# Four graph layers on one core: all units as one stream of chunk pairs, with tails and next queries emitted step by step between VectorE's passes

## Chip, cores, metric

One core of one Trainium2 chip. The metric is the device time of one execution in microseconds (us). All runs quoted here are in the fast state, so no difference below comes from a slower state of the chip. Experiments came on three chips; each was timed against the kernel before on its own chip. Engine names as in the profile: PE is TensorE (PEld its weight loads), DVE VectorE, ACT ScalarE, POOL GpSimd. L571 is line 571 of the kernel profiled.

## What is computed

16 graphs share one random adjacency matrix of 1024 nodes (density 1/128) and have 128 features each. Four layers run one after the other: layers 0, 2 and 3 are attention over the neighbours (8 heads of 16) with a feed-forward part, layer 1 is a simpler graph attention with one score per edge.

```python
def attention_layer(adj, h, ...):                   # L0, L2, L3
    Q, K, V = h @ Wq, h @ Wk, h @ Wv                # 8 heads of 16
    s = einsum(Q, K) / sqrt(16);  s = where(adj == 0, -inf, s)
    x = layer_norm(h + softmax(s) @ V @ Wo + bo)
    return layer_norm(x + relu(x @ W1 + b1) @ W2 + b2)
def graph_layer(x, adj, ...):                       # L1
    h = x @ W;  e = leaky_relu(h @ a_src [:, None] + h @ a_dst [None, :])
    e = where(adj == 0, -inf, e)
    return layer_norm(softmax(e) @ h + x)
```

## The kernel before

Nodes are sorted by degree. Keys and values (the graph layer: features and a score) are written per layer to a table in DRAM, and rows are fetched with indirect DMAs, here called **gathers**. A **chunk** is one gathered row for each of 128 places: four neighbours of 32 nodes. A **unit** is one layer, one half of the graphs, one tile of 128 nodes: 64 units. A unit has between 3 and 10 **pairs of chunks**; a pair is one gather buffer, `[128, 2, 2048]` floats in an attention layer. Before its passes a unit needs its **query replicas**: each node's query, copied to the places of its four neighbours. The unit's end, here called the **tail**, runs once for each of two halves `h` of four graphs. Cut to what the argument touches:

```python
def attention(l, g, t):
    # query, replicated over the rows of a chunk: PE, then ACT copies
    for h in range(HF): ...                 # q = x @ Wq;  qr[j//2][:, j%2, cols] = rep_j @ q
    for r, n in enumerate(ROUNDS[t]):
        for jp in range((n + 1) // 2):
            e, m = gathered(l, g, t, r, jp)                               # POOL issues
            nc.vector.tensor_tensor(e[..ROW], e[..ROW], qr[jp], ALU.mult)   # DVE 2.29 us
            nc.vector.tensor_reduce(sc, e[..ROW], X, ALU.add)               # DVE 2.28 us
            nc.scalar.activation(x, sc, AF.Exp, scale=...)                  # ACT
            nc.vector.tensor_tensor(v, v, x, ALU.mult)                      # DVE 2.28 us
        summed(t, r, acc, pairs, ROW)                                       # PE
    rec = divisors(t, es_by_round, G * H)
    for h in range(HF):                     # the tail of each half, in one go
        o = acc * rec;  oT = turned(o);  ps = oT @ Wo + x (by the identity)
        nc.vector.tensor_tensor(y, ps, bo, ALU.add);  z = normed(y)
        x1 = turned(z); f1 = relu(x1 @ W1 + b1); ps = f1 @ W2 + x1 (by the identity)
        nc.vector.tensor_tensor(y, ps, b2, ALU.add)
        finish(l, g, t, h, normed(y), ...)  # next layer's projection, or the output

def normed(y):
    ... bn_stats, bn_aggr on DVE -> mv
    nc.gpsimd.tensor_scalar(rstd, mv[:, :, 1], EPS, None, ALU.add)
    nc.gpsimd.tensor_tensor(rstd, rstd, power, ALU.pow)
    nc.vector.scalar_tensor_tensor(shift, mv[:, :, 0], -1.0, rstd, ALU.mult, ALU.mult)
    ... z = y * rstd + shift on ACT
# driver: for each layer, graph half and tile: attention(l, g, t) or graph_attention(l, g, t)
```

Of the kernel before, what the change touches and what calls it, by code (L numbers as in the profile page):

```python
# [20 lines left out]
P = 128  # L21
# [40 lines left out]
NC = len(CHUNK)  # L62

# [9 lines left out]
def sparse_path(ctx: ExitStack, tc: tile.TileContext, a: dict, out: bass.AP, flag):  # L73
# [227 lines left out]
    gathers = ctx.enter_context(tc.tile_pool(name="gathers", bufs=4))  # L301
    reps = ctx.enter_context(tc.tile_pool(name="reps", bufs=2))
# [3 lines left out]
    exps = ctx.enter_context(tc.tile_pool(name="exps", bufs=7))  # L306
# [7 lines left out]
    srcs = {}  # L314

    def project(l, g, t, h):

        table = tables[l, g][t * P : (t + 1) * P, :]
        if LAYERS[l][1] is ATTN:
            kv = twos.tile([P, 2, GH, D], F32, tag="kv", name="kv")  # L320
            for i in range(0, GH, 2):
                ps = bank([P, 2, 2 * D])
                for k in range(2):
                    nc.tensor.matmul(  # L324
                        ps[:, k, :], xT[g, t, h][:, i + k, :], w[LAYERS[l][0], "Wkv"],
                        start=True, stop=True,
                    )
                nc.scalar.copy(
                    kv[:, :, i : i + 2, :].rearrange("p c g d -> p g c d"),
                    ps.rearrange("p g (c d) -> p g c d", d=D),  # L330
                )
            nc.sync.dma_start(
                table.rearrange("p (c x) -> p c x", c=2)[:, :, h * GH * D : (h + 1) * GH * D],
                kv.rearrange("p c g d -> p c (g d)"),
            )
            return
# [3 lines left out]
        for i in range(0, GH, 2):  # L340
# [7 lines left out]
            nc.vector.tensor_copy(  # L348
# [3 lines left out]
            nc.vector.tensor_copy(  # L352
                srcs[g, t][:, at : at + 2].rearrange("p (g o) -> p g o", o=1), ps[:, :, D + 1 :]
            )

# [3 lines left out]
    def normed(y):  # L359
# [3 lines left out]
        for i in range(GH):  # L363
            nc.vector.bn_stats(st[:, i, :], y[:, i, :])  # L364
            nc.vector.bn_aggr(mv[:, i, :], st[:, i, :])  # L365
# [4 lines left out]
        nc.vector.scalar_tensor_tensor(shift, mv[:, :, 0], -1.0, rstd, ALU.mult, ALU.mult)  # L370
# [21 lines left out]
    def gathered(l, g, t, r, jp):  # L392
        n = min(2, ROUNDS[t][r] - 2 * jp)
        width = tables[l, g].shape[1]
        e = gathers.tile([P, 2, width], F32, tag="e", name="e")
        for k in range(n):
            nc.gpsimd.indirect_dma_start(  # L397
                out=e[:, k, :], out_offset=None, in_=tables[l, g][:, :],
                in_offset=bass.IndirectOffsetOnAxis(ap=idx[:, t, 2 * jp + k, r : r + 1], axis=0),
            )  # L400
        return e, n

    def summed(t, r, acc, es, base):

        n = ROUNDS[t][r]
        for h in range(HF):
            for j in range(n):
                nc.tensor.matmul(  # L408
                    acc[32 * j : 32 * j + 32, h, :],
                    marks[:, CHUNK[t, r, j], :],  # L410
                    es[j // 2][:, j % 2, base + h * GH * D : base + (h + 1) * GH * D],
                    start=(r == 0), stop=last_round(t, j) == r,
                )

    def last_round(t, j):
        return max(r for r, n in enumerate(ROUNDS[t]) if n > j)

    def divisors(t, ps_by_round, width):
        den = accs.tile([P, width], F32, tag="den", name="den")
        for r, n in enumerate(ROUNDS[t]):  # L420
            for j in range(n):
                nc.tensor.matmul(  # L422
                    den[32 * j : 32 * j + 32, :], marks[:, CHUNK[t, r, j], :],
                    ps_by_round[r][:, j, :],
                    start=(r == 0), stop=last_round(t, j) == r,
                )
        both = smalls.tile([P, 2, width], F32, tag="both", name="both")
        nc.scalar.copy(both[:, 0, :], den)
        nc.vector.reciprocal(both[:, 1, :], both[:, 0, :])
        nc.gpsimd.tensor_tensor(seen[:, :, :width], seen[:, :, :width], both, ALU.add)  # L430
        return both[:, 1, :]

    def attention(l, g, t):
        layer = LAYERS[l][0]
        p = {n: w[layer, n] for n in ("Wq", "Wo", "bo", "W1", "b1", "W2", "b2", "ln1_g", "ln1_b", "ln2_g", "ln2_b")}
        xt = [xT[g, t, h] for h in range(HF)]
        qr = [reps.tile([P, 2, ROW], F32, tag="qr", name="qr") for _ in range(J // 2)]
        for h in range(HF):
            q = ones_.tile([P, GH * D], F32, tag="q", name="q")
            ps = bank([P, GH, D])  # L440
            for i in range(GH):
                nc.tensor.matmul(ps[:, i, :], xt[h][:, i, :], p["Wq"], start=True, stop=True)
            nc.scalar.copy(q, ps.rearrange("p g d -> p (g d)"))
            cols = slice(h * GH * D, (h + 1) * GH * D)
            pss = []
            for j in range(J):
                ps = bank([P, GH * D])
                nc.tensor.matmul(ps, rep_of(j), q[32 * j : 32 * j + 32], start=True, stop=True)
                pss.append(ps)
            for j in range(J):  # L450
                nc.scalar.copy(qr[j // 2][:, j % 2, cols], pss[j])  # L451

        acc = accs.tile([P, HF, GH * D], F32, tag="acc", name="acc")
        es_by_round = []
        for r, n in enumerate(ROUNDS[t]):
            ex = exps.tile([P, J, G * H], F32, tag="ex", name="ex")
            pairs = []
            for jp in range((n + 1) // 2):
                e, m = gathered(l, g, t, r, jp)
                nc.vector.tensor_tensor(  # L460
                    e[:, :m, :ROW], e[:, :m, :ROW], qr[jp][:, :m, :], ALU.mult
                )
                sc = smalls.tile([P, 2, G * H], F32, tag="sc", name="sc")
                nc.vector.tensor_reduce(  # L464
                    sc[:, :m, :],
                    e[:, :m, :ROW].rearrange("p k (a d) -> p k a d", d=HD),
                    mybir.AxisListType.X, ALU.add,
                )
                x = ex[:, 2 * jp : 2 * jp + m, :]
                nc.scalar.activation(x, sc[:, :m, :], AF.Exp, scale=1.0 / HD**0.5)  # L470
                v = e[:, :m, ROW:].rearrange("p k (a d) -> p k a d", d=HD)
                nc.vector.tensor_tensor(  # L472
                    v, v,
                    x.rearrange("p k (a o) -> p k a o", o=1).to_broadcast([P, m, G * H, HD]),
                    ALU.mult,
                )
                pairs.append(e)
            summed(t, r, acc, pairs, ROW)
            es_by_round.append(ex)
        rec = divisors(t, es_by_round, G * H)  # L480
        xnew = []
        for h in range(HF):
            o = twos.tile([P, GH, D], F32, tag="o", name="o")
            nc.vector.tensor_tensor(
                o.rearrange("p g (a d) -> p (g a) d", d=HD),
                acc[:, h, :].rearrange("p (a d) -> p a d", d=HD),
                rec[:, h * GH * H : (h + 1) * GH * H]
                .rearrange("p (a o) -> p a o", o=1)
                .to_broadcast([P, GH * H, HD]),
                ALU.mult,  # L490
            )
            oT = twos.tile([P, GH, P], F32, tag="oT", name="oT")
            turned(o, oT)
            ps = bank([P, GH, D])
            for i in range(GH):
                nc.tensor.matmul(ps[:, i, :], oT[:, i, :], p["Wo"], start=True, stop=False)  # L496
                nc.tensor.matmul(ps[:, i, :], xt[h][:, i, :], ident, start=False, stop=True)  # L497
            y = twos.tile([P, GH, D], F32, tag="y", name="y")
            nc.vector.tensor_tensor(y, ps, over_graphs(p["bo"]), ALU.add)  # L499
            z = normed(y)  # L500
            x1 = twos.tile([P, GH, P], F32, tag="oT", name="x1")
            turned(z, x1, p["ln1_g"], p["ln1_b"])
            f1 = ones_.tile([P, F, GH * P], F32, tag="f1", name="f1")
            for f in range(F):
                ps = bank([P, GH * P])
                nc.tensor.matmul(  # L506
                    ps, p["W1"][:, f * P : (f + 1) * P], x1.rearrange("p g n -> p (g n)"),
                    start=True, stop=True,
                )
                nc.scalar.activation(f1[:, f, :], ps, AF.Relu, bias=p["b1"][:, f : f + 1])  # L510
            ps = bank([P, GH, D])
            for i in range(GH):
                for f in range(F):
                    nc.tensor.matmul(  # L514
# [531 lines left out]
```

## Time and profile before

| | before |
|---|---|
| time, median of 4 runs | 5873.0 us (5865.0 to 5879.9) |
| profiled span, mean clock of PE | 5874.2 us, 0.69 |
| PE, DVE, ACT, POOL busy | 52, 43, 21, 21% |
| unit of 4 pairs, attention | 95.6 us, DVE busy 36.6 |

The prediction reads one unit closely. Two more views are needed for what follows. The first is the table of windows with one line for each layer (columns: window; length; busy us and number of instructions of PE, PEld, DVE, ACT, POOL; clock; DMA share; GB/s). The layers end where VectorE takes the last reciprocal of their last unit; the first begins with the first large pass.

```profile
334.00:1921.70 1587.70, 820.65 (x3376) 426.14 (x3376) 710.85 (x1023) 335.16 (x705) 284.93 (x296) 0.67 0.29 110
1921.70:2672.90 751.20, 439.70 (x1846) 235.63 (x1848) 300.41 (x655) 143.63 (x358) 236.38 (x246) 0.67 0.42 138
2672.90:4308.60 1635.70, 843.18 (x3456) 429.45 (x3448) 703.15 (x927) 358.96 (x726) 296.37 (x307) 0.70 0.31 116
4308.60:5811.90 1503.30, 754.87 (x3184) 371.96 (x3184) 707.60 (x947) 308.59 (x652) 376.14 (x379) 0.67 0.31 119
```

The list of waits (who waited for what: total us, times, longest us):

```profile
DVE y L520 <- PE ps L518: 1005.5, 96, 11.3
DVE e L460 <- ACT qr L451: 650.4, 48, 189.1
DVE y L499 <- PE ps L497: 502.0, 96, 9.9
```

These are the two y steps of the tails and the query replicas: 2158 us of VectorE's idle time, 189 of them the one wait at the start.

### The profile page before, as it was taken

The numbers are of one execution on the slowest core, as the hardware profiler recorded it, in microseconds if no ns is written. First come the engines' busy times: TensorE is split into PE (matmuls) and PEld (weight loads), VectorE is DVE, ScalarE is ACT, GpSimd is POOL, SyncE is SP. The second block draws the span as 40 slices with busy tenths as digits, with TensorE's granted clock in tenths as the row PEclk, the third lists the DMA queues.
The fourth block names the chain that finished last, engine by engine and source line by source line (L and its number), as shares of the span: only waits on it lengthen the run. The fifth ranks groups of instructions, "written<-read, shape, count | busy, mean of one in ns | idle before, by whom it ended". The sixth has DMA issues, their size and how long they took to land.

```text
span 5874.2 us, 35428 instructions
## 1 busy us (share of the span) xinstructions
PE 3047.3 (52%) x12557; PEld 1603.2 (27%) x12557; DVE 2530.3 (43%) x3776; ACT 1229.9 (21%) x2588; POOL 1230.6 (21%) x1274
## 2 busy tenths in 40 slices
PE   2655554555555655565545555455555544545454
PEld 2422232322323323232222232222221222212222
DVE  6044534364343443445353424543335454363543
ACT  0222122211212112111222222122221212212122
POOL 0111211122111232332111111121112222232221
PEclk9766666666666666666767777677766666666666
DMA  1542423143231343535223123331314232143321
GB/s 35 197 161 91 149 84 118 50 155 146 86 118 58 98 147 137 166 133 204 97 108 135 72 108 132 123 142 72 125 69 183 107 140 97 75 182 118 132 76 50
DMA packets 142984, 686.89 MB, mean 117 GB/s; under 512 B 21200, under 2 KB 25040, under 8 KB 79824
## 3 DMA queue, kind: packets, MB, share of 16 engines
q0 software_dynamic: 99072, 619.38, 28.7%
q1 hardware_dynamic: 43728, 65.17, 3.0%
q8 instruction: 102, 1.67, 0.1%
q14 instruction: 82, 0.67, 0.0%
HBM read 617.31 MB, written 67.17 MB: 117 GB/s over the span
## 4 chain that ended last, share of the span: by engine, by line
PE 32%; DVE 30%; issue 10%; ACT 10%; POOL 8%; DMA 6%; POOLq 0%; DVEq 0%; ACTq 0%
DVE sc L464 8%; DVE e L460 7%; PE ps L383 6%; PE ps L506 6%; DVE e L472 6%; DMA e<-table,idx 5%; PE ps L324 4%; POOL rstd L368 4%; PE ps L514 3%; POOL e L397 3%; PE acc L408 3%; DVE st L364 3%; DVE e L547 2%; ACT qr L451 2%; ACT z L373 2%
## 5 line engine op out<-in xcount | busy, mean ns | idle before, releaser
L397 POOL DMA_INDIRECT e<-table,idx x656 | 803.3, 1225 | 1959.4 <-DVE e L460 1268.0
L408 PE MATMUL acc<-e,marks 128*32 128x512 f32 x2624 | 864.0, 981 | 397.1 <-DVE e L472 320.9
L460 DVE TENSOR_TENSOR e<-e,qr 128x2048 f32<-128x2048 f32 (+1 forms) x258 | 556.8, 2187 | 679.1 <-ACT qr L451 650.4
L383 PE MATMUL ps<-ident,z 128*128 128x128 f32 x768 | 312.1, 472 | 912.0 <-ACT z L373 911.5
L373 ACT ACTIVATE z<-y,shift,rstd 128x128 f32<-128x128 f32 x896 | 368.8, 482 | 1449.7 <-DVE shift L370 1449.7
L472 DVE TENSOR_TENSOR e<-e,ex 128x2048 f32<-128x2048 f32 (+1 forms) x258 | 555.6, 2184 | 12.6 <-ACT ex L470 12.6
L464 DVE TENSOR_REDUCE sc<-e 128x128 f32<-128x2048 f32 (+1 forms) x258 | 554.2, 2178 | 1.2
L422 PE MATMUL den<-ex,marks 128*32 128x64 f32 (+1 forms) x1312 | 120.0, 275 | 811.6 <-ACT ex L470 785.1
L520 DVE TENSOR_TENSOR y<-ps,b 128x512 f32<-128x512 f32 x96 | 66.4, 691 | 1005.5 <-PE ps L518 1005.5
L367 POOL TENSOR_SCALAR rstd<-mv 128x4 f32<-128x4 f32 x224 | 51.5, 230 | 2047.1 <-DVE mv L365 2046.5
L383 PEld LDWEIGHTS ps<-ident,z 128*128 128x128 f32 x768 | 138.9, 181 | 1082.3 <-ACT z L373 1082.3
L506 PE MATMUL ps<-x,W 128*128 128x512 f32 x384 | 361.0, 1094 | 83.4 <-ACT x L387 83.4
L470 ACT ACTIVATE ex<-sc 128x128 f32<-128x128 f32 (+1 forms) x258 | 78.5, 304 | 1417.8 <-DVE sc L464 1417.8
L324 PE MATMUL ps<-Wkv,xT 128*128 128x256 f32 x768 | 330.7, 605 | 77.6 <-ACT xT L387 55.6
L408 PEld LDWEIGHTS acc<-e,marks 128*32 128x32 f32 x2624 | 128.6, 144 | 875.4 <-DVE e L472 523.6
L422 PEld LDWEIGHTS den<-ex,marks 128*32 128x32 f32 x1312 | 59.1, 134 | 1083.5 <-ACT ex L470 1027.3
L514 PE MATMUL ps<-W,f 128*128 128x128 f32 x1536 | 281.5, 298 | 33.4 <-ACT f L510 33.4
L514 PEld LDWEIGHTS ps<-W,f 128*128 128x128 f32 x1536 | 242.5, 209 | 157.4 <-ACT f L510 116.0
L499 DVE TENSOR_TENSOR y<-ps,bo 128x512 f32<-128x512 f32 x96 | 66.4, 691 | 502.0 <-PE ps L497 502.0
L324 PEld LDWEIGHTS ps<-Wkv,xT 128*128 128x128 f32 x768 | 224.3, 306 | 152.7 <-ACT xT L387 74.4
L368 POOL TENSOR_TENSOR rstd<-rstd,power 128x4 f32<-128x4 f32 x224 | 234.1, 1045 | 15.2
L496 PE MATMUL ps<-Wo,oT 128*128 128x128 f32 x768 | 197.8, 348 | 67.6 <-ACT oT L385 66.3
(117 smaller groups left out, 3624.5 us busy)
## 6 DMA issues: line engine op xcount, KB each, us to landing
table<-kv SPq DMA_DIRECT2D x96, 512.0 KB, 3.0
e<-table,idx POOLq DMA_INDIRECT x656
table<-kv SPq DMA_DIRECT2D x32, 256.0 KB, 2.0
edges<-in_adj SPq DMA_DIRECT2D x8, 512.0 KB, 4.4
W<-in_L_gnn_W SPq DMA_DIRECT2D x6, 128.0 KB, 2.6
table<-kv SPq DMA_DIRECT2D x32, 2.0 KB, 1.8
xg<-in_x,places POOLq DMA_INDIRECT x16
out<-outs,places POOLq DMA_INDIRECT x16
```

Source lines behind the costliest of these rows:

```text
L324: nc.tensor.matmul(ps[:, k, :], xT[g, t, h][:, i + k, :], w[LAYERS[l][0], "Wkv"], start=True, stop=True,)
L368: nc.gpsimd.tensor_tensor(rstd, rstd, power, ALU.pow)
L373: nc.scalar.activation(z[:, i, :], y[:, i, :], AF.Identity, bias=shift[:, i : i + 1], scale=rstd[:, i : i + 1],)
L383: nc.tensor.transpose(ps[:, i, :], z[:, i, :], ident)
L397: nc.gpsimd.indirect_dma_start(out=e[:, k, :], out_offset=None, in_=tables[l, g][:, :], in_offset=bass.IndirectOffsetOnAxis(ap=idx[:, t, 2 ...
L408: nc.tensor.matmul(acc[32 * j : 32 * j + 32, h, :], marks[:, CHUNK[t, r, j], :], es[j // 2][:, j % 2, base + h * GH * D : base + (h + 1) * ...
L460: nc.vector.tensor_tensor(e[:, :m, :ROW], e[:, :m, :ROW], qr[jp][:, :m, :], ALU.mult)
L464: nc.vector.tensor_reduce(sc[:, :m, :], e[:, :m, :ROW].rearrange("p k (a d) -> p k a d", d=HD), mybir.AxisListType.X, ALU.add,)
L472: nc.vector.tensor_tensor(v, v, x.rearrange("p k (a o) -> p k a o", o=1).to_broadcast([P, m, G * H, HD]), ALU.mult,)
L496: nc.tensor.matmul(ps[:, i, :], oT[:, i, :], p["Wo"], start=True, stop=False)
L506: nc.tensor.matmul(ps, p["W1"][:, f * P : (f + 1) * P], x1.rearrange("p g n -> p (g n)"), start=True, stop=True,)
L514: nc.tensor.matmul(ps[:, i, :], f1[:, f, i * P : (i + 1) * P], p["W2"][:, f, :], start=(f == 0), stop=False,)
```

## The change

The intent is to put those waits of one unit under the passes of the next. The loop over units becomes one list of 344 pairs. Tails and queries become Python generators that stop (`yield`) after each stage, and between VectorE's passes there is a slot in which every open generator moves on by one stage. The order of the program is fixed. Two more things changed: within a unit the pairs go chunk pair by chunk pair and not round by round, and the divisors' sums are made with each pair and not at the unit's end. Core of the diff (unchanged arithmetic left out):

```diff
+AHEAD = 3
-            nc.vector.tensor_copy(kv[...scores...]); nc.vector.tensor_copy(srcs[...])
+            nc.scalar.copy(kv[...scores...]);        nc.scalar.copy(srcs[...]);  yield
-        nc.vector.scalar_tensor_tensor(shift, mv[:, :, 0], -1.0, rstd, ALU.mult, ALU.mult)
+        nc.gpsimd.tensor_tensor(shift, mv[:, :, 0], rstd, ALU.mult)
+        nc.gpsimd.tensor_scalar(shift, shift, -1.0, None, ALU.mult)
-    def attention(l, g, t): ...
-    def graph_attention(l, g, t): ...
+    def attention_tail(l, g, t, h, o):      # a yield after each stage
+        ...; y = ps + bo; stats = statistics(y); yield; z = normed(y, *stats); yield; ...
+    def queries(u): ...                     # a yield after each group of copies
+    def others():                           # one stage of each open tail, and of the query
+        advance(tails); advance(fronts) or advance(slow)
+    with tc.manual_schedule():
+        for i in range(len(pairs) + 1):
+            products(i)                     # graph layer: exponentials(i)
+            if closing is not None: ...     # divide the unit that ended; its tails open
+            others()
+            weighted(i - 1)
+            others();  exponentials(i)      # attention: reduce on DVE, Exp on ACT
+            summed(i - 1)
+            gathered(i - 1 + AHEAD)
+            others()
```

## The prediction

> **What bounds the kernel now.** I read the page first, then the table of windows over one whole unit (a unit is one layer, one half of the graphs, one tile of 128 nodes; there are 4 x 2 x 8 = 64), then VectorE's timeline inside it, then the groups by form. The page says that no engine is full and that the last-ending chain changes engine all the time:
>
> ```profile
> PE 3047.3 (52%) x12557; PEld 1603.2 (27%) x12557; DVE 2530.3 (43%) x3776; ACT 1229.9 (21%) x2588; POOL 1230.6 (21%) x1274
> ...
> PE 32%; DVE 30%; issue 10%; ACT 10%; POOL 8%; DMA 6%; POOLq 0%; DVEq 0%; ACTq 0%
> ```
>
> The fullest engine is busy half the time, and the chain is split between PE and DVE: they take turns. The windows put two consecutive units with 4 pairs of chunks side by side (columns: length, busy time of each engine, granted clock, DMA share, GB/s):
>
> ```profile
> 4003.75:4099.35 95.60, 49.63 (x208) 26.56 (x208) 36.53 (x57) 22.59 (x45) 15.38 (x17) 0.71 0.26 99
> 3908.00:4003.75 95.75, 52.95 (x218) 27.32 (x214) 36.71 (x58) 22.54 (x45) 18.50 (x20) 0.73 0.36 132
> ```
>
> A unit takes 95.6 us, in which DVE works 36.6 and PE some 51 (at a clock of 0.72). VectorE's timeline of the next unit shows where the rest goes:
>
> ```profile
> 4119.13 4.48 DVE L472 TENSOR_TENSOR e<-e,ex 128x2048 f32<-128x2048 f32 x2
> ...
> 4131.35 0.69 DVE L499 TENSOR_TENSOR y<-ps,bo 128x512 f32<-128x512 f32 x1 [3.48 <-PE ps L497]
> ...
> 4146.79 0.69 DVE L520 TENSOR_TENSOR y<-ps,b 128x512 f32<-128x512 f32 x1 [10.39 <-PE ps L518]
> ...
> 4160.72 0.69 DVE L499 TENSOR_TENSOR y<-ps,bo 128x512 f32<-128x512 f32 x1 [9.73 <-PE ps L497]
> ...
> 4174.82 0.69 DVE L520 TENSOR_TENSOR y<-ps,b 128x512 f32<-128x512 f32 x1 [10.53 <-PE ps L518]
> ...
> 4192.71 4.49 DVE L460 TENSOR_TENSOR e<-e,qr 128x2048 f32<-128x2048 f32 x2 [14.31 <-ACT qr L451]
> ```
>
> The three big passes of a unit (multiply by the query, reduce, weight by the exponential) end at 4123.6. Then the tail (output product, norm, feed-forward, norm, projection) runs for half 0 and, behind it, for half 1, as one chain through PE, ACT, DVE and POOL: four waits of about 10 us. Then DVE waits 14 us for the next query replicas. From 4123.6 to 4192.7 is 69 us in which DVE does about 10. The kernel is bound by latency, and another unit's passes could fill the gap.
>
> [...] (2286, 2277 and 2282 ns by form; start to start 2.20). The change does not touch these passes: they are the floor. [...] its clock records have only 0.5 and 1.0, mean 0.69, and eight L324 matmuls take 1.99 us in some places and 3.78 in others. [...] of 656 gather issues, those that meet no large tensor_tensor take 0.94 us, and one that starts under one waits for its end:
>
> ```profile
> L397 POOL DMA_INDIRECT e<-table,idx x656: 932/948/4052, 240.5 to 5738.0; - x164
> ```
>
> (min, median, max ns; 3.07 us is common.) [...]
>
> **The change, part by part.**
>
> *Passes and order.* The emission becomes one stream of 344 pairs. In each step DVE gets products(i), weighted(i-1), reduce(i), and between these stand three slots. In each slot the two tails of the previous unit and the preparation of the next unit's query go one stage forward. The order listing of the built program confirms it: in L2 DVE has multiply, weight, reduce, with the y and statistics groups singly between. So both 10 us waits and 14 us waits get other work over them, and a unit should tend to its longest engine instead of the sum.
>
> *DVE's own work.* 2530 us, of which 97 is in the first 200 us of set-up: 2433 in the stream. Removed: 128 small copies of the graph layer move to ACT (10.2 + 9.6 = 20 us), `shift` moves to POOL (36 us). Grouping the statistics changes little. Left: about 2380 us. By layer that is about 36 us for a 4-pair unit (36.6 less 4 x 0.16).
>
> *PE's work.* In the 4-pair unit 51 us x 0.72 = 37 us of full-clock work; from fast-state durations I get 34: per half 3 transposes 1.7, Wo 1.9, W1 1.75, W2 2.7, projection 2.0, so 20 for two; queries 5.8; four pairs at about 2.0. With PE more than 70% full, I expect it to stay at the fast clock (in this trace the records at full clock have a median busy share of 0.89 in the 3.4 us before, those at half 0.29). Whole kernel: 3047 x 0.69 = 2100 us. PE is then just below DVE: it is hidden only if the order lets it run ahead.
>
> *Replicas.* The old code issues four replica matmuls together (1.18 us for eight records); the new one two, so about 0.9 x 4 against 1.2 x 2: +1.2 us of PE per unit, included above.
>
> *POOL.* 656 gathers at 1.25 (0.94 and 0.30 between) = 820 us; 224 statistics at 0.23 + 1.05 + two new small ones at an estimated 0.22 each = 385; with the rest some 1330 us before any blocking.
>
> *Start and end.* In the old kernel both halves' first projections run before the first pass at 334 us. Now only half 0 does (8 tiles at 11 us from 134, then one query): first pass at about 236. The 80 us of the other half go under layer 0. After the last pair, nothing covers the last tail: about 45 us.
>
> *Sum.* Perfect overlap: 236 + 2380 + 45 = 2660 us. It will not be perfect. DVE and PE are nearly balanced, each queue is in order, and a y step that finds its PSUM tile unfinished stops the passes behind it. With 3 slots a pair, a 4-pair unit has 12 slots, a tail of the second half wants 14, so some is flushed together; the 3-pair unit has 9. I choose 25% on DVE's 2380 (about 600 us of stalls, some 45 us for the 4-pair unit): 236 + 2975 + 45 = 3256, so 3250 us.
>
> **The rivals.**
>
> *PE becomes the bound at the half clock.* If gaps keep it at 0.7, its 3047 us plus about 60 for the replicas come back in order, most of the span: 236 + 2900 + about 15% of stalls = 3550 to 3650. For it: busy 51 against 36.6 in the unit now. Against: that time is slow because PE waits; denser work should raise the clock.
>
> *POOL is locked out.* In a step two of DVE's three big passes (4.4 us) have two SBUF inputs. Open are the reduce (2.2) and the tail steps (about 2.8 per pair in a 4-pair unit), 5.0 against a need of 2.5 for two gathers and 1.7 for the statistics. It fits, barely; in a 10-pair unit 3.3 against 3.2. In the graph layer a pair has one 2.29 pass and only 0.35 open, so gathers may set its pace: about 5 us a pair where DVE needs 2.65. If every gather took 2 us: 1300 us on POOL, still hidden; if the statistics wait too, ACT and PE stall behind them: 3500 or more. The trace has no statistics step under a large pass, so this is not decided by it.
>
> *Transfers.* 687 MB; the 16 engines were busy 32% of 5874 = 1880 us. In a 3200 us span that is 59%, with buffers filled three pairs ahead. In a 10-pair unit a pair's 2.1 MB take 5.4 us at the best 20 us mean I worked out of the packet records (388 GB/s) against 6.6 of DVE, so it should hide. I give it little weight.
>
> *Near-perfect overlap.* Stalls of 8% give about 2850.
>
> *Little gained.* Only if the fixed order makes a chain that runs once through all engines in each step. Against it: tail stages are a slot apart, at least one 2.2 us pass, and most stages are 1 to 2 us long.
>
> **Range and chances.** The floor of 2660 is worked out from unchanged instructions, so I do not go much under 2850; the PE and POOL rivals reach 3650. The old unit must lose only 2% for "faster", and 69 of 96 us were open to be filled: 0.98 faster, 0.01 each for the others. 3250 us is 45% less than 5875.
>
> **What would show it right or wrong.** DVE busy at 2400 to 2480 us and 73 to 80% of the span; a 4-pair attention unit at 42 to 48 us; first large pass near 236 us; mean clock 0.85 or above; POOL busy at 1500 to 1900 with the median gather above 1.2 us; the longest waits now DVE on PE's y tiles and PE on ACT's z, each of 1 to 4 us instead of 10. PE stretched by the half clock would show as PE over 85% busy at 0.7. The lock would show as gathers and statistics of 2 to 4 us and ACT waiting on POOL. A DVE wait on gathers outside the graph layer would prove the transfer view wrong. I would be wrong altogether if DVE is under 60% busy: then the order itself makes the chain.

What is cut from this text are passages that no run here shows. The sum stands at 236 + 2380 + 45 = 2660 us, and with 25% on the middle term at 3256, so 3250. What is left of the paragraph with the cuts is read from the trace of the kernel before. The first bracket gives the lengths of VectorE's large multiply, reduce and weighting pass, on 2048 elements per partition. The clock records are TensorE's: 686, each 0.5 or 1.0, in steps of 3.41 us. TensorE was busy 0.89 (median) of the 3.41 us before a step at full clock and 0.29 before one at half; that it would stay at the fast clock when more than 70% full is the estimate from these two. Of the 105 gather issues that start under a large `tensor_tensor`, 100 take over 1 us; the median of the 105 is 2.82. The 161 that start under a large reduce take 0.94 in the median. That a queue works in order, which the sum uses, is shown by later runs for VectorE (it stood still 223.8 us in 223 waits ahead of an instruction of 0.16 us in e1, and 24.2 when that was emitted one pass later, e15) and for ScalarE (e8, exponentials behind a late z: 69 to 230 us); for TensorE it was not tested by itself.

## The result, and the profile after

The change took the time from **5873.0 to 3502.4 us** (median of 4 runs, 3491.5 to 3516.6). The ratio is 0.5965, 95% interval 0.5942 to 0.5989. Here and below a ratio is the mean time of one kernel's fast runs over that of the kernel before's fast runs of the same rounds, so it is not quite the ratio of the medians quoted. Where an experiment is set against the changed kernel, it is by the quotient of their two ratios.

The page's busy line, then its line of granted clocks (tenths, in 40 slices):

```profile
PE 2498.1 (72%) x12557; PEld 1416.2 (41%) x12557; DVE 2470.3 (71%) x3424; ACT 1182.6 (34%) x2716; POOL 1940.7 (56%) x1722
...
PEclk9978888888888988888788998888988787877787
```

The clock's mean rose from 0.69 to 0.84, so PE lost 549 busy us with the same 12,557 matmuls (busy time times clock is 2103 us before and 2098 after). DVE lost only 60 us: nearly all the gain is idle time. POOL alone got busier, by 710 us. By layer, in the same columns as before:

```profile
243.10:1127.40 884.30, 687.77 (x3567) 393.97 (x3568) 680.45 (x845) 346.98 (x856) 491.63 (x422) 0.84 0.60 218
1127.40:1681.50 554.10, 384.02 (x1896) 197.78 (x1895) 298.02 (x615) 145.84 (x391) 322.86 (x320) 0.85 0.58 192
1681.50:2521.80 840.30, 675.44 (x3425) 380.91 (x3423) 685.69 (x865) 336.15 (x716) 497.31 (x427) 0.86 0.62 226
2521.80:3440.20 918.40, 625.27 (x3152) 345.06 (x3153) 697.28 (x871) 293.54 (x644) 590.77 (x498) 0.80 0.51 192
```

The three attention layers gave 703, 795 and 585 us, the graph layer 197, the start 91 and the end 13: together the 2384 us between the spans. Length over DVE's busy time is now 1.30, 1.86, 1.23 and 1.32. Two layers stand out. The graph layer has the worst ratio. The last layer is 78 us longer than layer 2 with almost the same DVE work and less PE work.

VectorE's timeline over a unit of 4 pairs shows the interleaving (start us, us, instruction, in brackets the idle time before it):

```profile
2392.03 2.28 DVE L571 TENSOR_TENSOR e<-e,qr 128x2048 f32<-128x2048 f32 x1
2397.80 0.55 DVE L630 RECIPROCAL both<-both 128x64 f32<-128x64 f32 x1 [3.49 <-ACT both L628]
...
2408.81 0.69 DVE L436 TENSOR_TENSOR y<-ps,bo 128x512 f32<-128x512 f32 x1 [0.71 <-PE ps L433]
...
2422.03 0.69 DVE L463 TENSOR_TENSOR y<-ps,b 128x512 f32<-128x512 f32 x1 [2.58 <-PE ps L460]
...
2427.25 0.69 DVE L463 TENSOR_TENSOR y<-ps,b 128x512 f32<-128x512 f32 x1 [1.17 <-PE ps L460]
...
2436.29 2.29 DVE L571 TENSOR_TENSOR e<-e,qr 128x2048 f32<-128x2048 f32 x1 [0.59 <-DMA e<-table,idx]
```

Where the unit before had four y waits of 3.5 to 10.5 us and one of 14 for the replicas, there are now waits of at most 3.5 us. Units of 4 pairs take 44 to 47 us in layers 0 and 2 and 41 to 50 in the last layer (from reciprocal to reciprocal). But the list of waits has new entries at its top:

```profile
ACT z L382 <- POOL shift L376: 427.5, 129, 8.8
...
DVE e L571 <- DMA e<-table,idx: 304.3, 65, 99.0
...
PEld ps L392 <- ACT z L382: 244.2, 343, 4.5
...
DVE y L463 <- PE ps L460: 181.1, 89, 11.8
DVE sc L585 <- DMA e<-table,idx: 178.7, 46, 8.1
```

The y wait fell from 1005 to 181 us and the replica wait is gone. VectorE's longest waits are now for gathers: 178.7 us in the graph layer, and 205 in the attention layers (304.3 less 99.0 at the start, where nothing is there yet). Why are gathers late? The first norm instruction on POOL, before (L367) and after (L372), shows it (min/median/max ns, first and last start, form):

```profile
L367 POOL TENSOR_SCALAR rstd<-mv x224: 227/229/249, 405.8 to 5859.9; 128x4 f32<-128x4 f32 x112
```

```profile
L372 POOL TENSOR_SCALAR rstd<-mv x224: 222/2170/2343, 342.4 to 3474.2; 128x4 f32<-128x4 f32 x112
```

The same instruction, with four numbers per partition, went from 0.23 to 2.17 us in the median. Before, the tail ran alone, and none of the 224 started under a large `tensor_tensor`; now it runs under VectorE's large passes: 134 of the 224 start under a large `tensor_tensor` and end 0.08 to 0.10 us after it, 2.17 us in the median; the 46 that start under a large reduce take 0.23. Gathers show the same: 186 start under a large `tensor_tensor`, and 182 of them take over 1 us; the median is 2.4, and 41 take 5.3, under two such passes in a row. Under a large reduce the median stays at 0.95. And the gathers stand behind the statistics in GpSimd's queue: in the place below, in the graph layer, the next one starts at 1282.42, after statistics that began at 1276.97 (POOL, then DVE in the second fence):

```profile
1276.97 2.18 POOL L372 TENSOR_SCALAR rstd<-mv 128x4 f32<-128x4 f32 x1 [2.79 <-DVE mv L370]
1279.23 1.04 POOL L373 TENSOR_TENSOR rstd<-rstd,power 128x4 f32<-128x4 f32 x1
1280.34 1.28 POOL L375 TENSOR_TENSOR shift<-mv,rstd 128x4 f32<-128x4 f32 x1
...
1282.42 1.09 POOL L563 DMA_INDIRECT e<-table,idx  x1 [0.47 <-issue]
```

```profile
1289.32 0.18 DVE L585 TENSOR_TENSOR sc<-e,of 128x16 f32<-128x16 f32 x1 [7.75 <-DMA e<-table,idx]
```

The last layer has one thing more on POOL, the products with the output's gain and shift, and there both sides get longer. The 16 of these 64 products that start under a large `tensor_tensor` take 3.19 to 3.32 us, those that meet none 1.26 in the median; the large `tensor_tensor` passes that meet one take up to 3.38 us, those that meet none 2.28 in the median and 2.35 at most. POOL first, then VectorE's pass of the same moment:

```profile
2712.02 3.19 POOL L413 TENSOR_TENSOR outs<-outs,ln_b 128x512 f32<-128x512 f32 x1
```

```profile
2714.01 3.35 DVE L599 TENSOR_TENSOR e<-e,ex 128x2048 f32<-128x2048 f32 x1
```

### The profile page after: what moved, and what is told of

It is laid out like the page before. It is cut to its first block, busy times and chain, and to the rows that moved or that the text cites. A ratio compares the mean times of both kernels' runs of the same rounds, so it can differ in the third digit from the quotient of the medians.

```text
span 3489.8 us, 35525 instructions
## 1 busy us (share of the span) xinstructions
PE 2498.1 (72%) x12557; PEld 1416.2 (41%) x12557; DVE 2470.3 (71%) x3424; ACT 1182.6 (34%) x2716; POOL 1940.7 (56%) x1722
## 5 line engine op out<-in xcount | busy, mean ns | idle before, releaser
L563 POOL DMA_INDIRECT e<-table,idx x656 | 992.7, 1513 | 513.5 <-PE acc L619 206.1
L599 DVE TENSOR_TENSOR e<-e,ex 128x2048 f32<-128x2048 f32 (+1 forms) x344 | 761.3, 2213 | 71.9 <-ACT ex L583 69.0
L571 DVE TENSOR_TENSOR e<-e,qr 128x2048 f32<-128x2048 f32 (+1 forms) x258 | 568.4, 2203 | 317.6 <-DMA e<-table,idx 304.3
L372 POOL TENSOR_SCALAR rstd<-mv 128x4 f32<-128x4 f32 x224 | 315.6, 1409 | 474.7 <-DVE mv L370 451.3
L382 ACT ACTIVATE z<-y,shift,rstd 128x128 f32<-128x128 f32 x896 | 368.3, 482 | 433.4 <-POOL shift L376 427.5
L392 PE MATMUL ps<-ident,z 128*128 128x128 f32 x768 | 196.3, 340 | 185.6 <-ACT z L382 153.1
L373 POOL TENSOR_TENSOR rstd<-rstd,power 128x4 f32<-128x4 f32 x224 | 307.5, 1373 | 18.7
L550 ACT COPY qr<-ps 128x512 f32<-128x512 f32 x384 | 201.4, 591 | 182.2 <-PE ps L545 182.1
L326 PE MATMUL ps<-Wkv,xT 128*128 128x256 f32 x768 | 222.0, 434 | 40.6 <-ACT xT L396 21.7
L545 PE MATMUL ps<-q,rep 32*128 32x512 f32 x768 | 217.7, 662 | 2.8 <-ACT kv L330 2.5
L368 DVE BATCH_NORM_STATS2 st<-y 128x6 f32<-128x128 f32 x896 | 195.4, 281 | 7.6
L447 PE MATMUL ps<-x,W 128*128 128x512 f32 x384 | 190.1, 618 | 0.9 <-ACT x L396 0.9
```

The costliest lines, as they stand in the source:

```text
L326: nc.tensor.matmul(ps[:, k, :], xT[g, t, h][:, i + k, :], w[LAYERS[l][0], "Wkv"], start=True, stop=True,)
L382: nc.scalar.activation(z[:, i, :], y[:, i, :], AF.Identity, bias=shift[:, i : i + 1], scale=rstd[:, i : i + 1],)
L392: nc.tensor.transpose(ps[:, i, :], z[:, i, :], ident)
L545: nc.tensor.matmul(ps, rep_of(j), q[32 * j : 32 * j + 32, cols], start=True, stop=True)
L563: nc.gpsimd.indirect_dma_start(out=es[i][:, k, :], out_offset=None, in_=tables[l, g][:, :], in_offset=bass.IndirectOffsetOnAxis(ap=idx[:, ...
L571: nc.vector.tensor_tensor(e, e, qs[u, jp][:, :n, :], ALU.mult)
```

## The experiments

Theory A: what is left above the predicted 3256 us is GpSimd's queue: statistics blocked under VectorE's passes, and gathers behind them. Rival B: the gaps are TensorE's work and the fixed order, and the gathers would be late anyway. Rival C: gather bandwidth.

| run | change to the changed kernel | us, median of 4 | ratio to before | against changed |
|---|---|---|---|---|
| e1_stats_act | statistics POOL to ACT and DVE | 3465.3 | 0.5892 | -1.2% |
| e2_outs_dve | last products POOL to DVE | 3460.7 | 0.5886 | -1.3% |
| e5_tails_serial | tails run to their end at once | 4360.8 | 0.7427 | +24.5% |
| e8_gather_first | gather earlier in each step | 3638.9 | 0.6187 | +3.7% |
| e6_queries_serial | query at its unit's start | 3658.3 | 0.6232 | +4.5% |
| e10_pe_less | 1536 matmuls left out (wrong result) | 3400.3 | 0.5785 | -3.0% |
| e12_graph_ring | graph layer: two pairs per buffer | 3433.1 | 0.5837 | -2.1% |
| e16_z_later | z one slot later | 3580.7 | 0.6096 | +2.2% |
| e15_late_only | e1, its DVE step a slot later | 3304.0 | 0.5632 | -5.6% |
| e11_late_shift | e15 and e2 | 3280.4 | 0.5573 | -6.6% |
| e13_best | e11 and e12 | 3225.2 | 0.5484 | -8.1% |
| e17_best_order | e13, graph layer in another order | 3252.5 | 0.5532 | -7.3% |

All but e10 gave the right result. The half width of the 95% intervals of the ratios is 0.0010 to 0.0023.

### What the parts of the change were worth

**Tails at once.** Inside each of the changed kernel's steps nothing else moves, but the tails of a finished unit are emitted to their end before the next pass.

```diff
                 closing = None
+                while tails:
+                    advance(tails)
             others()
```

> Undoes one part: the tails of both halves are run to their end as soon as the unit's sums are divided, before the next VectorE pass, instead of one stage per slot. Queries of the next unit and the gathers stay ahead. If the interleaved tails are the main source of the gain: about 30 us more for each of 48 attention units and 12 for each of 16 graph units, so 4900 to 5300 us, DVE busy near 48%. If gathers and queries ahead are the main source: under 4000.

Measured 4360.8 us, between the two expectations: the interleaving of tails is worth 858 of the 2371 us, a good third, and neither "most" nor "little". VectorE's y waits come back, in part:

```profile
DVE y L463 <- PE ps L460: 443.4, 61, 10.3
...
DVE y L436 <- PE ps L433: 309.7, 96, 5.1
```

They are half of the 1507 us of the kernel before, because here the two halves still run side by side and gathers are on their way meanwhile.

**Queries at the unit's start.**

```diff
-                if jp == 0 and new and waiting:
-                    fronts.append(waiting.pop())
+                if new and i:
+                    for _ in queries(u): pass
-                if i == ends_of[u, 0] and u + 1 < len(units): ... fronts.append(queries(u + 1))
```

> The query part of the change is undone: a unit's query and its copies are made at once when the unit starts, not step by step in the unit before. In the chain of the kernel before the query to first product took about 11 us of each of 48 attention units. Theory: 48 x 8 to 13 us come back, 3880 to 4120 us. Rival (the tails alone fill the waits, and the query hides behind what they leave): 3500 to 3650 us.

Measured 3658.3 us, 156 more and just over the rival's range. The wait for replicas returns, but only at 291 us instead of 461 (650 less the start); the tails of the unit before now run in it. In the graph layer the wait for the score term comes back as well (75.5 us, L585 on L526), and the gather waits get shorter (219.7 and 115.1 us instead of 304.3 and 178.7):

```profile
DVE e L571 <- ACT qr L550: 291.4, 41, 18.0
```

The remainder, 2371 - 858 - 156 = some 1360 us, is what no single undo took away. Still in place in both runs are the overlapped passes of two pairs, the two halves' tails side by side, the gathers across unit borders and the earlier start (91 us). None of them was undone by itself, and the parts are not additive, so this is not a measured share of any of them.

### Is TensorE the bound?

```diff
-                nc.tensor.matmul(ps[:, i, :], oT[:, i, :], p["Wo"], start=True, stop=False)
-                nc.tensor.matmul(ps[:, i, :], xt[:, i, :], ident, start=False, stop=True)
+                nc.tensor.matmul(ps[:, i, :], oT[:, i, :], p["Wo"], start=True, stop=True)
     # the same with x1 after W2
```

> Wrong result on purpose: the two residual additions that TensorE does with the identity in the attention tails are dropped (768 + 768 matmuls, 169.7 + 148.7 = 318 us of TensorE's 2498). If TensorE's throughput bounds the attention layers, the time falls by 250 to 320 us, to 3180 to 3250. If VectorE with its waits bounds them and TensorE only lies on it at times (my theory: 2355 us of VectorE work in 3197 us), it falls by 40 to 130 us, to 3370 to 3460.

Measured 3400.3 us, 102 less and inside the range of "VectorE with its waits". But the test was smaller than planned, and it does not decide. The busy line of its page:

```profile
PE 2363.0 (70%) x11021; PEld 1247.3 (37%) x11021; DVE 2465.3 (73%) x3424; ACT 1191.1 (35%) x2716; POOL 1936.7 (57%) x1722
```

TensorE's busy time fell by 135 us (2498.1 to 2363.0) and not by 318: the busy times of lines overlap in the sum (in the changed kernel the lines add up to 2894 us, the engine was busy 2498), and the mean clock fell from 0.84 to 0.83. Against 135 us a gain of 102 is what a bound on TensorE could give too. The decision comes from e15 below. Its page has the same matmuls and almost the same busy time as the changed kernel, and it takes 198 us less:

```profile
PE 2470.4 (75%) x12557; PEld 1407.8 (43%) x12557; DVE 2490.4 (76%) x3649; ACT 1296.4 (39%) x3164; POOL 1266.0 (38%) x826
```

So TensorE's throughput is not what held the changed kernel at 3502 us. Its place in the chain still counts: in e10 the wait of the second y step falls from 181 to 137 us:

```profile
DVE y L461 <- PE ps L455: 137.0, 95, 11.3
```

### GpSimd's queue

**Statistics off POOL.** The power -1/2 becomes Exp(-Ln/2) on ScalarE, the shift one VectorE instruction. Both are out of GpSimd's queue.

```diff
-        nc.gpsimd.tensor_scalar(rstd, mv[:, :, 1], EPS, None, ALU.add)
-        nc.gpsimd.tensor_tensor(rstd, rstd, power, ALU.pow)
-        nc.gpsimd.tensor_tensor(shift, mv[:, :, 0], rstd, ALU.mult)
-        nc.gpsimd.tensor_scalar(shift, shift, -1.0, None, ALU.mult)
+        nc.scalar.activation(rstd, mv[:, :, 1], AF.Ln, bias=tiny[:, 0:1], scale=1.0)
+        nc.scalar.activation(rstd, rstd, AF.Exp, scale=-0.5)
+        nc.vector.scalar_tensor_tensor(shift, mv[:, :, 0], -1.0, rstd, ALU.mult, ALU.mult)
```

> Only edit: 1/sqrt(var + eps) is made on ACT (Ln with bias eps, then Exp with scale -0.5[...]) and the shift on DVE, so the four GpSimd instructions of each of the 224 statistics are gone. Theory A (GpSimd is held up by VectorE's two-input passes, and the statistics behind it stall ACT's z, PE's transposes and then DVE): the changed kernel's 3502 us fall to 3200 to 3350, DVE busy rises by about 36 us, ACT by about 90, the gathers' mean falls from 1.51 us, and the wait of ACT z on the shift falls from 428 us to under 200. Rival B (PE's in-order queue and clock set the stalls): 3480 to 3560, the extra small instructions cost a little.

Measured 3465.3 us. By the times theory A fell, and B was missed too, by 15 us. The waits say more:

```profile
DVE shift L378 <- ACT rstd L376: 223.8, 223, 3.0
DVE e L573 <- DMA e<-table,idx: 205.8, 37, 98.8
```

The gather waits fell by 98 us here and from 178.7 to 72.8 in the graph layer (L587). In their place came a new wait of about 1 us, 223 times: VectorE stands still until ScalarE has the root. The experiment had put in a wait as large as what it took out.

**The same, with VectorE's step a slot later.**

```diff
     def statistics(y):  ...
-        nc.vector.scalar_tensor_tensor(shift, mv[:, :, 0], -1.0, rstd, ALU.mult, ALU.mult)
-        return rstd, shift
+        return rstd, mv
-    def normed(y, rstd, shift):
+    def normed(y, rstd, mv):        # called one slot later, after another pass
+        nc.vector.scalar_tensor_tensor(shift, mv[:, :, 0], -1.0, rstd, ALU.mult, ALU.mult)
```

> Statistics on ScalarE and the late shift, with the last layer's products left on GpSimd. The last-layer products on VectorE gave 42 us in the last layer alone. If the rest of the 220 us is the late shift: 3305 to 3335 us. If the two need one another: over 3370 us.

Measured 3304.0 us, one us under the range. The wait is now this:

```profile
DVE shift L381 <- ACT rstd L376: 24.2, 51, 2.3
```

So the statistics on GpSimd cost the changed kernel 198 us (5.6%), within theory A's first range; 161 of them show only when no wait replaces them. By layer it is 60, 6, 60 and 61 us. GpSimd now stands idle in front of the gathers for 1003 us, until TensorE's sums free a buffer, instead of 293: the gathers no longer queue behind other work. The gathers themselves did not get shorter (1.63 us in the mean instead of 1.51, against theory A's mark). Theory A is thus right in that statistics hold up what stands behind them, and my first test of it was not clean. No run separates how much of the 198 us is the blocking under VectorE's passes and how much the statistics' unblocked length of about 1.7 us each.

**Last products off POOL.**

```diff
-        nc.gpsimd.tensor_tensor(o, z, over_graphs(gain), ALU.mult)
-        nc.gpsimd.tensor_tensor(o, o, over_graphs(shift), ALU.add)
+        nc.vector.tensor_tensor(...)    # the same two
```

> Only edit: the last layer's gain and shift products (64 instructions of 128x512) go from GpSimd to DVE. Theory A (in the last layer they stand in GpSimd's queue in front of the gathers and starve them: gaps of about 11 us before the product, one in each unit): the last layer falls from 919 us to about 830 to 860 although DVE gets 64 x 0.69 = 44 us more work; whole kernel 3420 to 3450. Rival B (PE order): DVE's extra 44 us add up, 3530 to 3550.

Measured 3460.7 us, 1.3% less, near A's range and far from B's. By the gap times, VectorE's idle time ahead of L571 in the last layer falls from 128 to 34 us, and the layer from 918 to 877 us (expected 830 to 860), although VectorE is busy 19 us more and waits 30 us for z ahead of the moved products. This also speaks against rival C: the last layer had the lowest DMA share of all, 0.51, and most of its gather wait went without a byte less to move.

**Both.**

> Statistics on ScalarE and last products on VectorE together (both already run singly: -1.2% and -1.3%), and the VectorE instruction that needs ScalarE's reciprocal root is emitted one slot later, after the next large pass. In the run with statistics on ScalarE VectorE waited 223.8 us for that root, in 223 waits. Theory: that wait was what ate the gain; without it 3200 to 3300 us. Rival: the wait moves to TensorE's y or to the gathers, 3400 to 3440 us, the sum of the two single gains.

Measured 3280.4 us, in the theory's range. In layer 2 (one window line, columns as above) VectorE is now busy 688 of 781 us, 88%, at a clock of 0.90:

```profile
1625.60:2406.80 781.20, 648.34 (x3427) 373.05 (x3425) 687.84 (x926) 367.89 (x841) 323.22 (x180) 0.90 0.67 243
```

**Gathers first.** If gathers are late, why not issue them at the head of the step?

```diff
             here = i < len(pairs)
+            if i:
+                gathered(i - 1 + AHEAD)
-            if i:
-                gathered(i - 1 + AHEAD)     # at its old place, after summed(i - 1)
```

> Only the order on GpSimd changes: the gather of pair i+2 is emitted at the start of step i instead of after its second slot, so statistics of the first two slots no longer stand before it. Theory A (gathers wait in GpSimd's queue behind held-up statistics): the 7.5 us gaps at the start of each graph unit and the last layer's 11 us gaps shrink, 3350 to 3450; statistics may come later instead and give some of it back. Rival B (PE order) or C (bandwidth): 3480 to 3520.

Measured 3638.9 us, 3.7% slower; all expectations missed. GpSimd's one queue carries both sorts of work, and what went ahead now holds up the other (427.5 and 69.0 us in the changed kernel):

```profile
ACT z L382 <- POOL shift L376: 569.6, 135, 7.5
...
DVE e L599 <- ACT ex L583: 230.4, 72, 13.4
```

ScalarE's z waits 142 us more for GpSimd, the exponentials behind z in ScalarE's queue come late, and VectorE waits 230 us for them instead of 69. The gather wait fell too (graph layer 178.7 to 74.2) and did not pay.

**z one slot later,** with the statistics left on GpSimd.

```diff
         stats = statistics(y)
         yield
+        yield
         z = normed(y, *stats)
```

> The changed kernel, with the normalisation z emitted one more slot after its statistics, which stay on GpSimd. Theory (z stands at the head of ScalarE's and then TensorE's queue and waits there 427.5 us for slow statistics; given one slot more, nothing waits for it): 3330 to 3420 us, and that wait below 150 us. Rival (the tails become so long that they are run to their end at the unit's end): 3500 to 3650 us.

Measured 3580.7 us, 2.2% slower. The wait that I wanted away is away, but VectorE waits for gathers instead:

```profile
DVE e L574 <- DMA e<-table,idx: 439.1, 84, 99.6
...
ACT z L382 <- POOL shift L376: 106.8, 44, 5.5
```

So taking away ScalarE's 427 us behind GpSimd, the largest entry but one of the list after the change, brought nothing: the gathers came later. The rival's number was right, its reason is not shown: units of 6 pairs (18 slots, where I count 16 for the longer tail) became longer too, 57 to 62 us, and those need not run their tails to the end. A slot's shift also moves the statistics against VectorE's passes and the gathers; which of these did it stays open.

### The graph layer

**Two pairs in one buffer.**

```diff
-        es[i] = gathers.tile([P, 2, width], F32, tag="e", name="e")
+        if is_attention(u): es[i] = gathers.tile([P, 2, width], F32, tag="e", name="e")
+        elif ring[i][1]:    es[i] = es_whole[0][:, 2:4, :]
+        else:               es_whole[0] = gathers.tile([P, 4, width], ...); es[i] = es_whole[0][:, 0:2, :]
-                gathered(i - 1 + AHEAD)
+                gathers_until(i - 2)    # all whose buffer was last used by a pair up to i - 2
```

> Only in the graph layer, two pairs of chunks share one gather buffer (a graph row is 1032 floats wide, half of an attention row), so that up to eight pairs can be on their way or in use instead of four; the attention layers keep their order. In the changed kernel the graph layer took 554 us (1127 to 1682 us) with VectorE busy 298 us and TensorE 384; a unit of four pairs took 27.5 us, thus 6.9 us per pair and 27.5 us for one round of the four buffers. Theory R (the round of a buffer is what the layer waits for: gather behind the statistics, landing, exponential, weighting, sums): the layer falls to 430 to 470 us and the whole to 3390 to 3430 us. Rival Q (order in the queues of TensorE and ScalarE: sums and exponentials stand behind tail steps): the layer stays over 530 us and the whole at 3480 to 3520 us.

Measured 3433.1 us, 2.1% less. In the profiled runs all of it lies in the graph layer, which took 500 us (columns as above); the wait for gathers ahead of the scores, 178.7 us, is no longer among the larger entries of the list of waits:

```profile
1133.10:1633.40 500.30, 378.22 (x1895) 198.75 (x1894) 295.97 (x614) 145.27 (x391) 314.55 (x316) 0.84 0.61 210
```

Neither range was met, R's by 3 us; in the layer theory R holds for 54 us, about half of what it expected. By unit: the two of 10 pairs fell from 66 and 54 to 59 and 37 us, those of 6 from 36 to 32, those of 4 stayed at 27. For the rest, rival Q has the trace on its side. In the combined kernel's graph layer, in a unit of 4 pairs:

```profile
1504.32 2.29 DVE L625 TENSOR_TENSOR e<-e,ex 128x2048 f32<-128x2048 f32 x1 [4.44 <-ACT ex L617]
...
1511.44 0.20 DVE L656 RECIPROCAL both<-both 128x8 f32<-128x8 f32 x1 [4.53 <-ACT both L654]
```

9 us of 27 go in two waits for ScalarE. In the first the exponential stands in its queue behind a tail's copy and four z steps; in the second ScalarE itself waits for TensorE's sums until just before.

**Combined.** e11's edits and e12's in one kernel.

> The kernel with late shift (3280 us) and the shared gather buffers of the graph layer (-70 us alone, all of it in that layer: 554 to 500 us). If the two are independent, since one acts mainly in the attention layers (graph layer 554 to 551) and the other only in the graph layer: 3200 to 3230 us. If what the buffers gave was waits behind the statistics on GpSimd, which are gone here: 3250 to 3290 us.

Measured 3225.2 us (3220.4 to 3231.5), in the first range: the two are close to independent (222 and 69 us singly, 277 together). This is the fastest kernel found, 45% under the kernel before and 8.1% under the changed one. Units of 4 pairs in layer 2 mostly take 37.7 us; the window over one of them:

```profile
2237.16:2274.88 37.72, 35.92 (x209) 22.13 (x209) 35.55 (x56) 23.19 (x53) 17.22 (x9) 1.00 0.76 276
```

PE is busy 35.9 us of it at the full clock and VectorE 35.5: in such a unit little is left to overlap. The DMA engines moved 276 GB/s in it and 243 over the layer, against 226 over the same layer of the changed kernel: bandwidth (rival C) was not what held that kernel's gathers there.

**Another order in the graph layer.** Both tail steps of a pair are emitted after its sums.

```diff
+            graph = here and not is_attention(u)
-            others()
+            if not graph: others()
             if i: weighted(i - 1)
             ...
             others()
+            if graph: others()
```

> The combined kernel (late shift, products on VectorE, shared graph buffers), and in the graph layer both tail steps of a pair are emitted after its sums, none before. In the shared-buffer run the graph layer took 500 us, TensorE busy 378, VectorE idle 204 of which 84.5 before the weighting (exponential late). If queue order is what is left there: graph layer 440 to 470 us, 30 to 60 us less than the combined kernel. If not: within 10 us of it or slower, since a tail gets its steps later.

Measured 3252.5 us, slower than the combined kernel by 0.9%. The wait ahead of the weighting did fall (80 to 57 us in the layer), but y waits for PE rose from 26 to 79. That order did not help does not show that order is not the matter: this one merely moved the wait from the exponential to y. What bounds those 27 us stays open between the two.

## Why the prediction was right, and where not

The prediction was 3250 us, range 2850 to 3650; measured 3502, so the call and the range held and the size was 7% low.

**What held.** The bound was latency, and it was filled: units of 4 pairs in layers 0 and 2 at 44 to 47 us (predicted 42 to 48), DVE busy 2470 (2400 to 2480), first large pass at 243 us (236), end 50 us (45). VectorE's large passes kept their length (2300, 2273, 2313 ns by form). TensorE's throughput is not the bound (e15), its busy share is 72% and not over 85, and its clock rose as it became denser (0.69 at 52% busy before), though to 0.84 and not 0.85.

**The step that failed is the Sum**, "I choose 25% on DVE's 2380", one stretch for all layers. In its own terms the stream had 2361 us of VectorE work: 1.25 times that is 2952, and it took 3197. The missing 245 us lie by layer (length less 1.25 times DVE busy) at +34, **+182**, -17 and +47. Layers 0 and 2 were sized right, within 17 us together, but in part by luck. The 25% was argued from VectorE and TensorE in balance and from y steps that find their PSUM tile unfinished; GpSimd's statistics stood outside the sum, as a rival. The two y waits make 72 of the 204 idle us in layer 0 and 62 of 155 in layer 2. With the statistics off GpSimd (e15) these layers take 825 and 781 us, 1.20 and 1.13 times VectorE's work: a cost that the sum did not contain filled what its allowance had too much. Three quarters of the miss is the graph layer, for which 1.25 was never argued: it has little VectorE work to hide behind. The text had the better number two paragraphs on, gathers at "about 5 us a pair" in that layer; 86 pairs make 430 us, measured 554 or 6.4 a pair. It was left out of the sum. Of the excess, the round of the buffers accounts for 54 us (e12); the rest is open. The trace points to the queues of ScalarE and PE, but only that one other order does not help is shown (e17). The last layer's 47 us are about what GpSimd's products cost there (e2: 42).

**The GpSimd rival** was named and half taken: "if the statistics wait too, ACT and PE stall behind them: 3500 or more", "not decided by" the trace. They did wait (2.17 us in the median), and it cost 198 us (e15). But it was not ACT's wait alone: 321 of its 427 us could be taken away with no gain while gathers came later (e16). The median gather did not pass the predicted mark of 1.2 us (0.95; the mean did, 1.51), and POOL's 1941 us passed its 1900.

**A mark that was wrong.** "A DVE wait on gathers outside the graph layer would prove the transfer view wrong." It came, 205 us, and proves nothing of bandwidth: it falls to 107 us (e2) and 121 (e15) when POOL is relieved. Here a wait on a DMA was also a wait on whatever stood ahead of its issue.

**DVE's share** of the span was 71%, under the predicted 73 to 80, by the same 245 us. The longest waits were not only y and z: VectorE's longest were for gathers.

**A line misread.** "Four waits of about 10 us" in the old tail are three (10.39, 9.73, 10.53) and one of 3.48. It does not enter the sum.

## What to carry to other kernels

When a kernel waits by turns on its engines, emitting the stages of independent work between the passes of the fullest engine can remove most of the wait (here VectorE's idle time fell from 3344 to 1020 us). Size the gain stage by stage: the stage with the least work on that engine keeps most of its waits (here the graph layer kept 256 of 451 idle us, layer 0 204 of 877). Afterwards look at the queue that issues the transfers, and keep small dependent instructions that get blocked out of it (here one took 2.17 us in the median instead of 0.23). When you move such an instruction, emit whatever waits for it one pass later, or the test may only trade one wait for another (here 223.8 us in e1, 24.2 in e15).
